# Image sums, spectra's first steps, the image load and the attention's add moved inside layer 0 of a two-layer Fourier and attention kernel

## The chip, the cores and the metric

The kernel runs on one core of one Trainium2 chip. The metric is device microseconds of one execution, given as the median of several runs. The profile is of one further execution.

## The reference

All data is float32; x is (4, 32, 128, 128). Two layers are added to x one after the other. Only the first concerns the change: it treats each of the 4 batch entries as 32 images of 128x128.

```python
x = x + _L0_conv_ref(_gn(x), ...)        # _gn: group norm over groups of 4 channels, whole batch entry
# inside _L0_conv_ref, xa = _gn(x) as 128 images of 128x128:
xn = _inorm(xa, norm1_w, norm1_b)        # _inorm: mean and variance of each image
k = _fno_layer(xn, Kcw, Ksw, Hs, Ws)     # truncated FFT, mode weights, inverse FFT, plus a skip
q = _fno_layer(xn, Qcw, Qsw, Hs, Ws)
v = _fno_layer(xn, Vcw, Vsw, H, W)
p_attn = softmax(q·k / sqrt(Hs*Ws))      # over the 32 images of a batch entry, per head
av = p_attn · v
p = _fno_layer(av, Pcw, Psw, H, W)
a = _inorm(p + xa, attn_w, attn_b)
an = _inorm(a, norm2_w, norm2_b)
m = _fno_layer(an, m0cw, m0sw, H, W, inner_norm=True, act=True)    # gelu
m = _fno_layer(m, m1cw, m1sw, H, W, inner_norm=True, act=False)
out = _inorm(m, mon_w, mon_b) + a
# second layer: t += attention(layer_norm(t)); t += mixture of 8 experts, top 2 (layer_norm(t))
```

## The kernel before

`layer0` runs over the four batch entries b, with the 32 images of one entry in SBUF as `xt`, 128 partitions (rows) by 32 x 128. FFTs are matmuls with cosine and sine tables. Means and variances are not taken from the images where their spectrum or sums give them, so that each normalisation becomes a scale and a bias of some later operation.

The body of iteration b has these stages, in the order of the program:

- **Load** of images b+1 (`load`, L122): four DMAs of 512 KB, two issued by SyncE (SP), two by ScalarE (ACT), at the head of the iteration. The pool `l0_x` has two buffers.
- **Value product** (L756 to L788): five blocks of columns of the modes (`NK` = 13 of 64 each). In a block, four pairs of DMAs on SP fetch `xb` (the spectra, replicated over partitions by a broadcast from DRAM; 8 DMAs of 214.5 KB to a block in all but the last, four buffers); POOL and DVE multiply by the weights `gb` (`u`, L773 and L775), and PE sums into `po`. After each block ACT copies `po` to `rs` (L788). Then `py` and `inverse` bring the result to image space and add it to `q`.
- **Statistics of q** (`stats`, `flat_part`, L831): mean and variance, and `q_r`, the inverse deviation, by `inv_std` (L204): Ln and Exp on ACT (L208, L209) between small DVE operations. `ra` is the scale of q, `r2` that of the second normalisation.
- **spectra(0, q)** (L852): `first_step` (PE `pz`, evacuated to `z1` by `evacuate`, L188 on ACT two times in three and L190 on DVE), then PE `px` (L871), `sqx` on ACT (L873), `part1`, `part2` on DVE (L879, L882), their sum on POOL (L885), a negated copy on ACT (L891).
- **v0's chain** (`weighed`, L894): the squares times a weight (L899), their row sum (L906), two small operations (L909, L915), a matmul `ms` with a matrix of ones; then `r0` by `inv_std`, and the scales `hq`, `hs0`, `hb` of gelu.
- **back(0)** (L290, twice, a half of the images each): PE `y1` (L297), evacuation `v1`, PE `four` (L308), and for each image `gelu`: DVE L941, ACT Gelu L944, DVE `bn_stats` L951. Behind each half, `add_attention` for 16 images: one DVE operation each (L848), `xr = q * ra + xr`, on the image tile of b itself.
- **image_sums(b+1)** (L320): squares of the images on ACT, row sums and square sums on PE (`rows8`, L330, 16 pairs of matmuls), `ev`, 16 small matmuls `s12`, then a chain of small operations over DVE, PE (`mg`, `bg`, `my`) and ACT (`gn_r`, `n1_r`, each an Ln and an Exp): group norm's scale and shift, and the first instance norm's scale `ysc`.
- **spectra(1, gl)** and **spectra_of_images(b+1)** (L418): for groups of 8 images a `first_step`, the correction for the group's mean (`less_mean`, two DVE operations), `px` (L263, L264) with the columns `colg` that hold the group norm's scale, `xx` on DVE, stores to `xd` by SP; at the end `xm` (ACT, L457).
- **v1's chain**, as v0's, to the scales `c2`, `c3` and the bias `cq`.
- **attention_weights(b+1)** (L491): 17 steps of products `pa` (DVE) and `pb` (DVE one time in three, else POOL L524, 12 of 17) and PE `sp`, then `spt`, scores, softmax, and `pr` by way of DRAM, with which the next value product begins.
- **The end of b**: ACT scales gelu's result (L999, Identity with a scale and a bias, 32 images), POOL adds four groups of 8 images to `xr` (L1006), `back(spec, a, last)` adds the rest, SP stores.

For b = 0 the image sums, the spectra and the attention weights run ahead of the loop, beside the preparation of the value weights. In the last iteration there is no next batch; the first part of layer 1 is begun in its place.

PSUM tiles have the tags `a`, `b` and `wide`, of two buffers each: `pz`, `po` and `pxt` are `a`; `px`, `py`, `sk` and `four` are `b`; `y1`, `xw`, `m`, `x0`, all `sums` and `rows8` are `wide`. In SBUF, tag `z` has two buffers, `pr` six.

The order within layer 0 isn't written by hand: a planner places each engine's instructions from the program's order, the dependencies and its own estimates of their durations. Once placed, each engine runs its instructions strictly in that order. Layer 1's attention is in an order written out by hand.

Of the kernel before, what the change touches and what calls it, by code (L numbers as in the profile page):

```python
# [13 lines left out]
P = 128  # L14
# [94 lines left out]
def layer0(  # L109
# [9 lines left out]
    ]  # L119
    const, ps, images, values, modes = (p.__enter__() for p in pools + right)  # L120

    def load(b):  # L122
        xt = images.tile([P, T, C], F32, name=f"x_{b}", tag="x")
        for g in range(0, T, GI):
            eng = nc.sync if g % 16 == 0 else nc.scalar
            eng.dma_start(out=xt[:, g : g + GI], in_=x[b, g : g + GI].rearrange("t w c -> w t c"))
        return xt

    def logarithms():
# [120 lines left out]
            if z.shape[2] > P:  # L250
                evacuate(z[:, k : k + 4, P:], pz[:, :, :64], -1.0)

    def forward(images, c1, c2, take, change):


        n = c1.shape[1]
        z = grp.tile([P, GI, 192], F32, name="z", tag="z")
        first_step(images, z)
        change(z)
        for k in range(0, GI, 4):  # L260
            px = ps.tile([P, 4, n], F32, name="px", tag="b")
# [46 lines left out]
            nc.tensor.matmul(four, inv, v, start=True, stop=True)  # L308
            take([image(a, g, k) for k in range(4)], four)

    def sums(name, matrix, src):

        m = ps.tile(list(src.shape), F32, name=name, tag="wide")
        nc.tensor.matmul(m, matrix, src, start=True, stop=True)
        return m

# [3 lines left out]
    def image_sums(b, xt):  # L320


        rows8 = ps.tile([64, 4, C], F32, name="rows8", tag="wide")
        for g in GROUPS:
            xx2 = grp.tile([P, GI, C], F32, name="xx2", tag="pr", bufs=6)
            nc.scalar.activation(xx2, xt[:, g : g + GI], AF.Square)
            for h in range(2):
                m = g // 4 + h
                for k, src in enumerate((xt[:, 4 * m : 4 * m + 4], xx2[:, 4 * h : 4 * h + 4])):
                    nc.tensor.matmul(  # L330
                        rows8[32 * k : 32 * k + 32],
                        one_of_8[:, 7 - m : 39 - m],
                        src,
                        start=m == 0,
                        stop=m == 7,
                    )
        ev = grp.tile([64, 4, C], F32, name="ev", tag="v", bufs=3)
        nc.scalar.copy(ev, rows8)
        s12 = ps.tile([P, 2, 512], F32, name="s12", tag="wide")[:, :, :T]
        for j in range(4):  # L340
            for k in range(2):
                r = slice(32 * k, 32 * k + 8)
                nc.tensor.matmul(s12[:, k, j::4], ev[r, j], ident[r, r], start=True, stop=True)
        sv = small.tile([P, 2, T], F32, name="sv", tag="pk_sq")
        nc.vector.tensor_copy(sv, s12)

        tot = one("tot", 2)
        nc.vector.tensor_reduce(tot, sv, AX.X, ALU.add)
        mg = sums("mg", group, tot)
        gm = one("gm")  # L350
        nc.vector.tensor_copy(gm, mg[:, 0:1])
        gv = one("gv")
        nc.vector.tensor_mul(gv, gm, gm)
        nc.vector.tensor_tensor(gv, mg[:, 1:2], gv, ALU.subtract)
        gr, _ = inv_std("gn_r", gv, 1)
        gs = one("gs")
        nc.vector.tensor_mul(gs, gm, gr)

        both = small.tile([P, 2, 32], F32, name="both", tag="both")
        nc.vector.tensor_scalar(both[:, 0], of_group, gr, None, ALU.mult)  # L360
        nc.vector.tensor_scalar(both[:, 1], of_group, gs, -1.0, ALU.mult, ALU.mult)
        by_group = small.tile([P, 2, 32], F32, name="by_group", tag="by_group")
        nc.vector.tensor_copy(by_group, sums("bg", ones, both))
        n = 1 + 2 * KY
        colg = small.tile([P, 2, n], F32, name="colg", tag="colg")
        nc.vector.tensor_scalar(colg[:, 0], cols1[:, :n], gr, None, ALU.mult)
        nc.vector.tensor_scalar(colg[:, 1], cols2[:, :n], gr, None, ALU.mult)
        m128 = one("m128")
        nc.vector.tensor_scalar(m128, gm, 128.0, None, ALU.mult)

        gs128 = one("gs128")
        nc.vector.tensor_scalar(gs128, gs, 128.0, None, ALU.mult)
        gg = one("gg")
        nc.vector.tensor_mul(gg, gs, gs128)
        gr2 = one("gr2")
        nc.vector.tensor_mul(gr2, gr, gr)
        grs = one("grs")
        nc.vector.tensor_scalar(grs, gs, gr, -2.0, ALU.mult, ALU.mult)
        y12 = small.tile([P, 2, T], F32, name="y12", tag="pk")
        nc.vector.tensor_scalar(y12[:, 0], sv[:, 0], gr, gs128, ALU.mult, ALU.subtract)  # L380
        nc.vector.tensor_scalar(y12[:, 1], sv[:, 1], gr2, gg, ALU.mult, ALU.add)
        nc.vector.scalar_tensor_tensor(
            y12[:, 1], sv[:, 0], grs, y12[:, 1], ALU.mult, ALU.add
        )
        nc.vector.tensor_scalar(y12, y12, 1.0 / NPIX, None, ALU.mult)
        my = sums("my", ones, y12)
        ym, yv = per_image("ym"), per_image("yv")
        nc.vector.tensor_copy(ym, my[:, 0])
        nc.vector.tensor_mul(yv, ym, ym)
        nc.vector.tensor_tensor(yv, my[:, 1], yv, ALU.subtract)  # L390
        yr, _ = inv_std("n1_r", yv)
        ysc = scalars(ALU.mult, "n1_s", yr, par[:, N1W : N1W + 1])
        return by_group, colg, m128, ysc

    prep_pool = tc.tile_pool(name="l0_prep", bufs=1)
    prep = prep_pool.__enter__()
# [21 lines left out]
    def spectra_of_images(b, xt, normed):  # L418


        _, colg, m128, ysc = normed
        n = 1 + 2 * KY
        xx = modes.tile([P, T, n], F32, name=f"xx_{b}", tag="xx")
        xd = dram.tile([T, 2, KX, KY], F32, name=f"xd_{b}")
        for g in GROUPS:

            def scaled(k, px):
                i = slice(g + k, g + k + 4)
                nc.vector.tensor_tensor(
                    xx[:, i], px, ysc[:, i].unsqueeze(2).to_broadcast([P, 4, n]), ALU.mult  # L430
                )

            def less_mean(z):
                nc.vector.tensor_scalar(z[:, :, 0], z[:, :, 0], m128, None, ALU.subtract)
                nc.vector.tensor_scalar(z[:, :, P], z[:, :, P], m128, None, ALU.add)

            forward([xt[:, g + t] for t in range(GI)], colg[:, 0], colg[:, 1], scaled, less_mean)

            i = slice(g, g + GI)

            for r, y in ((0, 1 + KY), (64, 1)):
                bias = par[r : r + 1, N1B : N1B + 1].to_broadcast([1, GI])
                nc.vector.tensor_copy(xx[r : r + 1, i, y], bias)
            for part in range(2):
                nc.sync.dma_start(
                    out=xd[i, part].rearrange("t x y -> x t y"),
                    in_=xx[64 * part : 64 * part + 64, i, 1 + KY :],
                )
# [238 lines left out]
    for b in range(B):  # L687
        xt = loaded
        by_group, _, _, ysc = normed
        xd = front[2]  # L690
        if b + 1 < B:
            loaded = load(b + 1)

        ph, pr = weights


# [54 lines left out]
        for x0 in range(0, KX, NK):  # L751
# [3 lines left out]
            for i in range(4):  # L755
                xb = late.tile([P, 2, NK * KY], F32, name="xb", tag="xb")[:, :, :m]  # L756
                for r in range(2):
                    nc.sync.dma_start(
                        out=xb[:, r],
                        in_=xd[8 * i : 8 * i + 8, r, x0 : x0 + nk]  # L760
                        .rearrange("s x y -> s (x y)")
                        .unsqueeze(1)
                        .to_broadcast([8, 16, m]),
                    )
# [20 lines left out]
                if i % 2 and at_c < C:  # L785
                    skips(at_c)
                    at_c += 16
            nc.scalar.copy(rs[:, x0 : x0 + nk].rearrange("p x y -> p (x y)"), po)  # L788
        if b + 1 == B:
            for p in reversed(right):  # L790
                p.__exit__(None, None, None)
# [52 lines left out]

        def add_attention(g):

            for t in range(g, g + GI):
                nc.vector.scalar_tensor_tensor(  # L848
                    xr[:, t], q[:, t], ra[:, t : t + 1], xr[:, t], ALU.mult, ALU.add
                )  # L850

        def spectra(layer, src):  # L852

# [78 lines left out]
        nc.vector.tensor_scalar(hb, hb, par[:, S0 : S0 + 1], None, ALU.mult)  # L932
        nc.vector.tensor_mul(dq, dq, hs0)
        nc.vector.tensor_tensor(hb, hb, dq, ALU.add)
        gl = big.tile([P, T, C], F32, name=f"g_{b}", tag="y")
        st = grp.tile([P, T, 6], F32, name="st", tag="st")
        for a in HALVES:
# [13 lines left out]
                    nc.vector.bn_stats(st[:, t], gl[:, t])  # L951

            back(spec, a, gelu)
            for g in (16 * a, 16 * a + GI):
                add_attention(g)

        logarithms()
        if b + 1 < B:
            normed = image_sums(b + 1, loaded)
        else:  # L960
            first((ps, images))

        glm, glv, flat = stats("gl", st)
# [1 line left out]
        dg = per_image("dq")  # L965
        nc.vector.tensor_copy(dg, d1)
        spec, sq = spectra(1, gl)
        if b + 1 < B:
            front = spectra_of_images(b + 1, loaded, normed)
        v1 = weighed("v1", sq, squares, layers[1][2])  # L970
# [675 lines left out]
```

## Time and profile before

| what | us |
| --- | --- |
| median of 3 runs | 3180.41 |
| lowest and highest | 3179.98, 3183.43 |
| profiled execution, its own time | 3191.62 |
| its span in the trace | 3189.9 |
| busy PE / DVE / ACT / POOL | 2928.7 / 2290.9 / 2311.7 / 2102.7 |
| mean granted TensorE clock | 0.953 |

In the profile, L12 is line 12 of the kernel before. "PE" are matmuls, "PEld" the loads of their weights, DVE is VectorE, ACT ScalarE, POOL GpSimd. Tenths of busy time are given for 40 equal slices of the span; "PEclk" is the clock that the throttle granted to TensorE, in tenths of full speed. In brackets behind an instruction stands how long its engine was idle before it, and what released it; "x16" are 16 instructions in a row of one line. The arrow in `out<-in` leads from the operands to the result.

### The profile page before, as it was taken

The page shows a single profiled execution, that of the slowest core. Times are in us where ns is not written, and L with a number is a line of the kernel's source. Part 1 is how long each engine was busy: PE and PEld are TensorE (multiplying, and loading weights), DVE is VectorE, ACT ScalarE, POOL GpSimd, SP SyncE. Part 2 cuts the span into 40 slices and gives each one's busy share as a digit, 9 for nine tenths or more (in the row PEclk, how much of TensorE's full clock was granted, in tenths as well). Part 3 has the DMA queues.
Part 4 walks back from the last instruction along what each step waited for, and adds up shares of the span by engine and source line. Part 5 has one row for each costly group of instructions (what it writes and reads, how often), then busy time and mean ns, then how long its engine had stood idle before and what let it go on. Part 6 is the DMA issues. An engine that isn't in the chain of part 4 may idle for free.

```text
span 3189.9 us, 53099 instructions
## 1 busy us (share of the span) xinstructions
PE 2928.7 (92%) x19634; PEld 1438.2 (45%) x19634; DVE 2290.9 (72%) x5035; ACT 2311.7 (72%) x3138; POOL 2102.7 (66%) x1831
## 2 busy tenths in 40 slices
PE   7888798798888789999999999999999999999997
PEld 5366365345546444444344443444444444444443
DVE  5876666667677566777666868866778777687887
ACT  2344243253343589998999999998999999999992
POOL 1621540460451289878788797889878889888773
PEclk6998998899898799999999999999999999999998
DMA  6301310130140211010111010011010011101000
GB/s 140 111 18 30 95 50 3 49 123 1 30 130 2 57 31 31 8 31 7 31 37 24 14 24 14 8 39 31 23 29 9 14 37 24 37 1 31 14 14 14
DMA packets 152308, 112.77 MB, mean 35 GB/s; under 512 B 36878, under 2 KB 140657, under 8 KB 151441
## 3 DMA queue, kind: packets, MB, share of 16 engines
q1 hardware_dynamic: 136209, 103.61, 12.2%
q10 hardware_dynamic: 15840, 5.77, 0.8%
q8 instruction: 155, 2.54, 0.3%
q14 instruction: 104, 0.85, 0.1%
HBM read 68.37 MB, written 20.00 MB: 28 GB/s over the span
## 4 chain that ended last, share of the span: by engine, by line
PE 61%; POOL 12%; ACT 9%; DVE 9%; issue 7%; DMA 1%; ACTq 0%; POOLq 0%; DVEq 0%; SPq 0%
PE d L1446 19%; PE po L1465 11%; PE px L1352 6%; ACT r L1496 4%; PE po L778 4%; PE n L1446 3%; POOL e L1505 3%; POOL e L1504 3%; PE pz L248 2%; PE four L308 2%; ACT e L1512 2%; PE px L871 1%; PE sk L742 1%; POOL kx L1111 1%; DVE r L1501 1%
## 5 line engine op out<-in xcount | busy, mean ns | idle before, releaser
L1501 DVE TENSOR_TENSOR r<-n,r 128x1024 f32<-128x1024 f32 (+1 forms) x1056 | 961.6, 952 | 479.0 <-PE n L1446 389.4
L1504 POOL TENSOR_TENSOR e<-r 128x512 f32<-128x512 f32 x528 | 673.2, 1275 | 268.1 <-DVE r L1501 267.6
L1496 ACT ACTIVATE r<-d 128x1024 f32<-128x1024 f32 (+1 forms) x1056 | 792.9, 802 | 67.4 <-PE n L1446 56.4
L1508 ACT ACTIVATE r<-r 128x1536 f32<-128x1536 f32 x528 | 783.6, 1484 | 16.8
L1505 POOL TENSOR_TENSOR e<-e,r 128x512 f32<-128x512 f32 x528 | 671.3, 1271 | 41.4
L1446 PE MATMUL d<-qe,ke 32*128 32x512 f32 (+3 forms) x2304 | 605.8, 602 | 39.6 <-ACT r L1496 36.5
L1465 PE MATMUL po<-e,kx 128*128 128x512 f32 (+3 forms) x1152 | 594.5, 605 | 15.6 <-POOL e L1517 15.6
L1446 PE MATMUL n<-qe,ke 32*128 32x512 f32 (+3 forms) x2304 | 606.2, 601 | 0.0
L1446 PE MATMUL n<-qf,kf 32*128 32x512 f32 (+3 forms) x2304 | 552.6, 554 | 0.0
L1446 PE MATMUL d<-qf,kf 32*128 32x512 f32 (+3 forms) x2304 | 550.2, 553 | 0.0
L1356 DVE SCALAR_TENSOR_TENSOR xc<-px,wgt,xc 128x128 f32<-128x128 f32 x1024 | 358.1, 350 | 42.2 <-PE px L1352 9.7
L1512 ACT ACTIVATE e<-e 128x512 f32<-128x512 f32 x528 | 325.8, 617 | 66.2 <-POOL e L1505 65.6
L1465 PEld LDWEIGHTS po<-e,kx 128*128 128x128 f32 x1152 | 175.5, 188 | 392.8 <-issue 306.9
L1446 PEld LDWEIGHTS d<-qe,ke 32*128 32x128 f32 x2304 | 176.5, 183 | 359.3 <-ACT r L1496 339.5
L773 POOL TENSOR_TENSOR u<-xb,gb 128x858 f32<-128x858 f32 (+1 forms) x120 | 233.1, 1968 | 139.5 <-PE po L778 128.0
L1446 PEld LDWEIGHTS d<-qf,kf 32*128 32x128 f32 x2304 | 220.2, 186 | 176.1 <-issue 163.8
L1352 PE MATMUL px<-we,x2t 128*128 128x512 f32 x512 | 264.0, 601 | 6.8 <-DVE xc L1356 6.0
L775 DVE TENSOR_TENSOR u<-xw,gb 128x858 f32<-128x858 f32 (+1 forms) x200 | 206.6, 1082 | 59.2 <-PE po L778 46.6
L885 POOL TENSOR_TENSOR spec<-part,part 128x512 f32<-128x512 f32 x16 | 24.8, 1550 | 333.4 <-ACT z L188 75.2
L1446 PEld LDWEIGHTS n<-qf,kf 32*128 32x128 f32 x2304 | 228.3, 185 | 19.2 <-issue 11.4
L778 PE MATMUL po<-u,pr 128*32 128x429 f32 (+1 forms) x1280 | 191.1, 548 | 26.8 <-DVE u L775 11.7
L524 POOL TENSOR_TENSOR pb<-xm 128x1024 f32<-128x1024 f32 x48 | 90.7, 1913 | 159.1 <-ACT xm L457 152.8
(388 smaller groups left out, 3953.9 us busy)
## 6 DMA issues: line engine op xcount, KB each, us to landing
xb<-xd SPq DMA_DIRECT2D x128, 214.5 KB
xc<-x SPq DMA_DIRECT2D x29, 512.0 KB
x<-x SPq DMA_DIRECT2D x16, 512.0 KB
qf<-qe SPq DMA_DIRECT2D x64, 128.0 KB
out<-xc SPq DMA_DIRECT2D x15, 512.0 KB
xb<-xd SPq DMA_DIRECT2D x32, 198.0 KB
gb<-gd SPq DMA_DIRECT2D x4, 1056.0 KB
x<-in_x SPq DMA_DIRECT2D x8, 512.0 KB
```

Of the source, the lines that this page charges most:

```text
L773: nc.gpsimd.tensor_tensor(u, xb, gk, ALU.mult)
L778: nc.tensor.matmul(po[32 * j : 32 * j + 32], pr[:, i, k], u[:, r], start=i == 0 and k == 0, stop=i == 3 and k == 1,)
L1352: nc.tensor.matmul(px, x2t[:, k * P : (k + 1) * P], we[:, e0 : e0 + 4], start=True, stop=True)
L1356: nc.vector.scalar_tensor_tensor(xc[:, k], px[:, e], wgt[:, k, e0 + e : e0 + e + 1], xc[:, k], ALU.mult, ALU.add)
L1446: nc.tensor.matmul(o, k, q, start=turn == 0 or g > 0, stop=turn == 1 or g > 0)
L1465: nc.tensor.matmul(sums[c, h][:, q0 : q0 + c1 - c0], kx[:, jb], e[:, c0:c1], start=jb == 0, stop=is_last and q0 > 2 * P, skip_group_check= ...
L1496: nc.scalar.activation(r[:, g], d, AF.Ln, scale=1.0 / DSCALE)
L1501: nc.vector.tensor_tensor(r[:, g], part, r[:, g], ALU.mult)
L1504: nc.gpsimd.tensor_tensor(e, r[:, 1], r[:, 2], ALU.add)
L1505: nc.gpsimd.tensor_tensor(e, e, r[:, 0], ALU.add)
L1508: nc.scalar.activation(r, r, AF.Exp, scale=-1.0)
L1512: nc.scalar.activation(e, e, AF.Exp)
```

## The change

- `image_sums(b+1)` is called before gelu's stage, behind v0's chain in the program. Its PSUM tiles take the tags `a` and `b` instead of `wide`, and `s12` becomes two tiles, copied by two operations.
- The four DMAs that load images b+1 are issued in the second of the value product's five blocks, all on SP, with an ordering dependency behind the last broadcast of that block.
- In `spectra_of_images` the first step of a group of 8 images is put ahead of the `px` of the group before it. The correction for the mean is one DVE operation for a group instead of two.
- `add_attention` becomes, for 8 images, eight scaled copies on ACT and one addition on POOL. Its calls stand behind `spectra(1, gl)`, where the program had them behind each half of gelu's stage.

```diff
-    def load(b):
+    def load(b, behind=None):
...
-            eng = nc.sync if g % 16 == 0 else nc.scalar
-            eng.dma_start(out=xt[:, g : g + GI], in_=x[b, g : g + GI].rearrange("t w c -> w t c"))
+            eng = nc.sync if behind is not None or g % 16 == 0 else nc.scalar
+            d = eng.dma_start(
+                out=xt[:, g : g + GI], in_=x[b, g : g + GI].rearrange("t w c -> w t c")
+            )
+            if behind is not None:
+                tc.add_manual_dep(
+                    d.ins,
+                    behind.ins.name,
...
-    def forward(images, c1, c2, take, change):
+    def forward(z, c1, c2, take):
...
-        z = grp.tile([P, GI, 192], F32, name="z", tag="z")
-        first_step(images, z)
-        change(z)
...
-    def sums(name, matrix, src):
+    def sums(name, matrix, src, tag="wide"):
...
-        rows8 = ps.tile([64, 4, C], F32, name="rows8", tag="wide")
+        rows8 = ps.tile([64, 4, C], F32, name="rows8", tag="a")
...
-        s12 = ps.tile([P, 2, 512], F32, name="s12", tag="wide")[:, :, :T]
+        s12 = [ps.tile([P, T], F32, name=f"s{t}", tag=t) for t in "ab"]
...
-        nc.vector.tensor_copy(sv, s12)
+        for k in range(2):
+            nc.vector.tensor_copy(sv[:, k], s12[k])
...
-        mg = sums("mg", group, tot)
+        mg = sums("mg", group, tot, "a")
...
-        m128 = one("m128")
-        nc.vector.tensor_scalar(m128, gm, 128.0, None, ALU.mult)
+        shift = one("shift", 2)
+        for k in range(2):
+            nc.vector.tensor_scalar(shift[:, k : k + 1], gm, 256.0 * k - 128.0, None, ALU.mult)
...
         xd = dram.tile([T, 2, KX, KY], F32, name=f"xd_{b}")
-        for g in GROUPS:
+        steps = []
+        for g in (*GROUPS, None):
+            if g is not None:
+                z = grp.tile([P, GI, 192], F32, name="z", tag="z")
+                first_step([xt[:, g + t] for t in range(GI)], z)
+                nc.vector.tensor_tensor(
+                    z[:, :, ::P], z[:, :, ::P], shift.unsqueeze(1).to_broadcast([P, GI, 2]), ALU.add
+                )
+                steps.append((g, z))
+                if g == 0:
+                    continue
+            g, z = steps.pop(0)
...
-            def less_mean(z):
-                nc.vector.tensor_scalar(z[:, :, 0], z[:, :, 0], m128, None, ALU.subtract)
-                nc.vector.tensor_scalar(z[:, :, P], z[:, :, P], m128, None, ALU.add)
-
-            forward([xt[:, g + t] for t in range(GI)], colg[:, 0], colg[:, 1], scaled, less_mean)
+            forward(z, colg[:, 0], colg[:, 1], scaled)
...
         xd = front[2]
-        if b + 1 < B:
-            loaded = load(b + 1)
...
-                    nc.sync.dma_start(
+                    broadcast = nc.sync.dma_start(
                         out=xb[:, r],
...
             nc.scalar.copy(rs[:, x0 : x0 + nk].rearrange("p x y -> p (x y)"), po)
+            if x0 == NK and b + 1 < B:
+                loaded = load(b + 1, broadcast)
...
         def add_attention(g):
-            for t in range(g, g + GI):
-                nc.vector.scalar_tensor_tensor(
-                    xr[:, t], q[:, t], ra[:, t : t + 1], xr[:, t], ALU.mult, ALU.add
-                )
+            part = grp.tile([P, GI, C], F32, name="scaled_q", tag="pr", bufs=6)
+            for t in range(GI):
+                nc.scalar.activation(
+                    part[:, t], q[:, g + t], AF.Identity, scale=ra[:, g + t : g + t + 1]
+                )
+            nc.gpsimd.tensor_tensor(xr[:, g : g + GI], xr[:, g : g + GI], part, ALU.add)
...
         nc.vector.tensor_tensor(hb, hb, dq, ALU.add)
+        if b + 1 < B:
+            normed = image_sums(b + 1, loaded)
...
             back(spec, a, gelu)
-            for g in (16 * a, 16 * a + GI):
-                add_attention(g)
 
         logarithms()
-        if b + 1 < B:
-            normed = image_sums(b + 1, loaded)
-        else:
+        if b + 1 == B:
             first((ps, images))
...
         spec, sq = spectra(1, gl)
+        for g in GROUPS:
+            add_attention(g)
```

More of the change, by code (lines that the diff above doesn't have):

```diff
@@ L120, in layer0 @@
     const, ps, images, values, modes = (p.__enter__() for p in pools + right)
-    def load(b):
+    def load(b, behind=None):
         xt = images.tile([P, T, C], F32, name=f"x_{b}", tag="x")
         for g in range(0, T, GI):
-            eng = nc.sync if g % 16 == 0 else nc.scalar
-            eng.dma_start(out=xt[:, g : g + GI], in_=x[b, g : g + GI].rearrange("t w c -> w t c"))
+            eng = nc.sync if behind is not None or g % 16 == 0 else nc.scalar
[6 more added lines that the diff above has]
+                    behind.ins.name,
+                    mybir.DependencyInfo(mybir.DependencyClass.NoSync, mybir.DependencyReason.DATA),
+                    reason="order",
+                )
         return xt
@@ L309, in back @@
             take([image(a, g, k) for k in range(4)], four)
-    def sums(name, matrix, src):
-        m = ps.tile(list(src.shape), F32, name=name, tag="wide")
+    def sums(name, matrix, src, tag="wide"):
+        m = ps.tile(list(src.shape), F32, name=name, tag=tag)
         nc.tensor.matmul(m, matrix, src, start=True, stop=True)
@@ L342, in image_sums @@
                 r = slice(32 * k, 32 * k + 8)
-                nc.tensor.matmul(s12[:, k, j::4], ev[r, j], ident[r, r], start=True, stop=True)
+                nc.tensor.matmul(s12[k][:, j::4], ev[r, j], ident[r, r], start=True, stop=True)
         sv = small.tile([P, 2, T], F32, name="sv", tag="pk_sq")
-        nc.vector.tensor_copy(sv, s12)
+        for k in range(2):
+            nc.vector.tensor_copy(sv[:, k], s12[k])
         tot = one("tot", 2)
         nc.vector.tensor_reduce(tot, sv, AX.X, ALU.add)
-        mg = sums("mg", group, tot)
+        mg = sums("mg", group, tot, "a")
         gm = one("gm")
@@ L362, in image_sums @@
         by_group = small.tile([P, 2, 32], F32, name="by_group", tag="by_group")
-        nc.vector.tensor_copy(by_group, sums("bg", ones, both))
+        nc.vector.tensor_copy(by_group, sums("bg", ones, both, "a"))
         n = 1 + 2 * KY
@@ L385, in image_sums @@
         nc.vector.tensor_scalar(y12, y12, 1.0 / NPIX, None, ALU.mult)
-        my = sums("my", ones, y12)
+        my = sums("my", ones, y12, "a")
         ym, yv = per_image("ym"), per_image("yv")
@@ L392, in image_sums @@
         ysc = scalars(ALU.mult, "n1_s", yr, par[:, N1W : N1W + 1])
-        return by_group, colg, m128, ysc
+        return by_group, colg, shift, ysc
     prep_pool = tc.tile_pool(name="l0_prep", bufs=1)
@@ L418, in spectra_of_images @@
     def spectra_of_images(b, xt, normed):
-        _, colg, m128, ysc = normed
+        _, colg, shift, ysc = normed
         n = 1 + 2 * KY
```

## The prediction

> **What bounds the kernel now.** I read the page's busy tenths first, to see where TensorE is short of work and at which clock.
>
> ```profile
> PE   7888798798888789999999999999999999999997
> ...
> PEclk6998998899898799999999999999999999999998
> ```
>
> A slice is 79.75 us. Layer 0 is the first 14 slices (to 1106 us), where PE stands at 7 to 9 and the clock dips; layer 1 behind it is PE at 9 throughout, and the diff doesn't touch it. So all gain or loss lies in layer 0, between the end of one batch's value product and the start of the next, four times (q_r's Ln at 211.9, 470.4, 738.6, 1001.0 us). Next the windows of image batch 1 (columns: window, length, busy PE, PEld, DVE, ACT, POOL with counts, clock, DMA):
>
> ```profile
> 467.00:487.00 20.00, 13.49 (x152) 10.20 (x152) 17.11 (x60) 5.29 (x14) 3.44 (x2) 0.92 0.01 1
> 487.00:495.00 8.00, 6.18 (x70) 4.60 (x70) 6.58 (x33) 2.46 (x5) 0.00 (x0) 0.71 0.01 2
> 495.00:522.00 27.00, 27.00 (x111) 13.78 (x112) 16.27 (x64) 16.86 (x38) 0.00 (x0) 0.64 0.00 1
> 522.00:541.00 19.00, 18.31 (x169) 12.05 (x165) 9.79 (x51) 5.56 (x13) 1.27 (x1) 1.00 0.01 1
> 541.00:573.00 32.00, 28.61 (x226) 26.82 (x227) 19.33 (x64) 6.71 (x18) 1.27 (x1) 0.89 0.22 50
> 573.00:610.00 37.00, 27.79 (x174) 7.36 (x174) 28.43 (x34) 15.41 (x37) 33.30 (x17) 0.77 0.07 21
> ```
>
> In the first, PE waits and DVE is full; in the third PE is full at clock 0.64; the last is POOL's. The chain of waits for 467 to 573 says which piece ends each (start, length, what):
>
> ```profile
> 482.38 1.13 DVE sqx L899
> 483.51 1.27 DVE x L848
> 484.77 1.13 DVE v_r L906
> 486.75 0.65 PE ms L314 x2
> 488.68 0.78 DVE x L848 x3
> ...
> 519.10 5.27 PE rows L330 x22
> ```
>
> The attention's adds (L848) stand inside v0's chain, and the next batch's row sums (L330) inside gelu's stretch. The timelines of PE, POOL and ACT price the wait, the lock and what follows:
>
> ```profile
> 486.75 0.63 PE L314 MATMUL ms<-v_s,ones 128*128 128x32 f32 x2 [6.33 <-DVE v_s L915]
> 482.46 2.17 POOL L885 TENSOR_TENSOR spec<-part,part 128x512 f32<-128x512 f32 x1 [6.09 <-DVE part L882]
> 488.72 0.23 ACT L208 ACTIVATE r<-r_ve 128x32 f32<-128x32 f32 x1 [3.64 <-DVE r_ve L207]
> 492.99 1.08 ACT L188 ACTIVATE v<-y 128x512 f32<-128x512 f32 x2 [3.78 <-DVE v L190]
> 524.46 0.58 ACT L338 COPY ev<-rows 64x512 f32<-64x512 f32 x1 [1.66 <-PE rows L330]
> 537.81 0.22 ACT L208 ACTIVATE n_r<-n_r_ve 128x32 f32<-128x32 f32 x1
> ```
>
> **What the Trainium skill says.** "SBUF — State Buffer", "SBUF: two separate sides": a GpSimd operation and a VectorE operation with two SBUF inputs exclude each other. The trace agrees: L885 took 2.17 us where it met L899, 1.27 otherwise. "TensorE: Matmul & The Clock Gate", "Part 1: The HAM clock gate": the clock halves after an idle window and returns after about 3.4 us of sustained work. It agrees at 484 to 514; it doesn't at 32 to 66, where PE was busy with px and stayed at 0.5. "DMA: Bandwidth & Descriptors", "Issuing engines are not separate DMA queues": transfers of SP and ACT share the 16 engines. It agrees: batch 2's image load, half on each, delayed the xb behind it to 384.4 us.
>
> **The change, part by part.** The instruction order of the changed program shows where things stand. Batches 0, 1, 2 have all parts.
>
> *A, q_r to the first gelu* (25.7, 25.0, 26.0 us now). Removed: the 32 L848, 0.26 us apart on DVE; some 5 fall inside v0's links, about 1.4 us. Added on ACT: 32 copies. L999 with two pointers took 12.04/31 = 0.39 us each; by "ScalarE: Activation LUTs", "What ACT_TABLE_LOAD costs", a pointer less saves 0.09, so 0.30 to 0.39, 9.6 to 12.4 us; I take 12.4. ACT is busy 5.3 of 20 there, so 17.7 of 20: it fits, but sqx waits up to four copies (1.6 us), and r0's Ln stands behind all. Added on POOL: four adds, as L1006 2.36 us each, 9.4 us beside its 3.4; each can hold L899 or L909 up to 2.4 us. I take ms 2 us late, range 0 to 5. Then the image-sum chain: in the new ACT order ev, gn_r's and n1_r's Ln and Exp stand ahead of v1's first evacuation (L188) and the table load, and on DVE the chain's small operations ahead of its own share. ev to n1_r took 13.35 us above, of which about 4.3 were waits for foreign work on PE and DVE, so 9.1 alone. r0's Ln to evacuation took 4.3; now 9.1 + 0.5. So +5 more: **+7 a batch**, 4 to 10.
>
> *B, gelu's stretch* (19.2, 26.1, 19.0). The rows8 passes leave; 13 of 16 pairs now come ahead of ms, in the 6.3 us where PE waited (16 x 0.43 = 6.9). B1 lost most by half clock. −1, −6, −1, together **−8**, range −13 to −4.
>
> *C, last gelu to xm* (49.9, 51.4, 52.4). Gone: rows8's tail (1.3 to 3 us), ev and the sums' waits between spectra(1)'s passes: in batch 3, where nothing is interleaved, spectra(1) ends 17.8 us after gelu, against about 20. The images' transform then runs one group ahead, so px doesn't wait for its group's evacuation: 28.6 of 32 us were busy at clock 0.89, leaving 4 to 7. The mean's correction becomes one DVE operation in place of two, ahead of need. 2 + 4 + 5 = **−11 a batch**, range −13 to −8.
>
> *D, xm to spt to po* (36.8 + 27 to 30). POOL's ten pb products precede L1006, so they aren't held 2 x 2.36 us; but the last two stand behind the first L1006, which needs cq, whose chain on DVE moved behind xx. **+0.5 a batch**, range −3 to +2.5.
>
> *E, the load.* Four DMAs move, all on SP, behind the 16 broadcasts of the second K block; ACT's queue loses two. Batch 2's load cost the first xb 9.8 us in the chain at 375.9, part of it covered: that block ended 13.6 us after the start against 14.35 a block later. The load's 2.1 MB moves to the third block's broadcasts, prefetched further. −1.5 in batches 1 and 2; +1.5 in batch 0, where x_1 was loaded at the start. **−1.5**, range −6 to +6. The image sums have it from a block or more before they start.
>
> *F, batch 3*: no sums, only the swap of adds: A's part without the chain, **+2**, range −3 to +4.
>
> *G, the start.* The sums take PSUM's "a" and "b", so 64 passes that ran in the chain's waits (16 to 31 us) follow `my` (35.2): 64 x 0.116 = 7.4 us at full clock. px at half clock (32 to 66) would gain as much if these warm it; 16 passes of 8 images' px take 3.5 us against 6.8. Also x_1's half load leaves ACT's queue. **−2**, range −8 to +9.
>
> Sum: 21 − 8 − 33 + 1.5 − 1.5 + 2 − 2 = −20 us. The profiled execution had a span of 3189.9 and 3191.62 in all, so 3171.6 by its own clock; it lies 11.2 above the median of 3180.41, so **3160** there. The ends of A to G taken as independent: 9, 4.5, 7.5, 8, 6, 3.5, 8.5 in squares, about 18 us either way.
>
> **Rivals.**
> *R1, slower: the copies on ACT become the bound of part A.* If none of the 12.4 us hides (the copies run while sqx, spec and z1's evacuations are wanted), A is 12.4 + 6 = 18.4 a batch. The other parts give −41, so the sign turns at 13.7, and 0.2% slower from 15.8. At 18.4: +14, 3195. For it: ACT executes in order and r0's Ln stands last. Against it: ACT was idle 14.7 of the 20 us.
> *R2, no difference: part C isn't realised.* If PE, no longer held by the chain, waits for z's evacuation instead (L188 already ended 14.1 us of waits in 467 to 573), C is −4, and the sum +1: 3181. D at its upper end does half of this. Against it: DVE and ACT were 19 and 7 busy of 32.
> *R3, more:* the start warms and A is at its low end: −35, 3145.
> That the change doesn't do what it says is nearly excluded by the order; only the place of rows8's last three pairs is against the words.
>
> **The numbers.** Likeliest case 0.55, R3 0.12, R2 0.17, R1 0.16. About 0.2% (6.4 us) is what a measurement of this kernel can tell from no change. The likeliest and R3 are faster, with a quarter of R2: 0.71. R2's middle is same: 0.10. R1 and the rest slower: 0.19. The range 3138 to 3190 leaves out the lower half of R3 and the upper half of R1.
>
> **What would show it.** After: ms's idle below 6.3 us, with rows8 ahead of it; gelu's first activation 32 us after q_r's Ln (25 now); gelu's stretch near 19 in batch 1; last gelu to xm near 40; POOL's pb without a gap; the second K block's broadcasts without a 9.8 us piece. Wrong if the scaled copies end the wait of r0's Ln by several us (R1), if gelu to xm stays at 47 or more (R2), or if layer 1's part, 2084 us from 1106 to the end, changes by over 5.

## The result, and the profile after

The changed kernel is slower: a median of 3225.45 us (3219.59 to 3227.78, 4 runs) against 3181.92 us (4 runs) for the kernel before, a ratio of 1.0133 with a 95% interval of 1.0116 to 1.0151. The profiled execution of after took 3227.78 us, its span is 3226.1; the two spans differ by 36.2 us, somewhat less than the medians, since the profiled execution of before lay 11 us above its own median. Layer 1 took 2088.8 us from its table load at 1137.3 to the end, 2088.9 before (from 1101.0). So all of it is in layer 0.

The starts and ends of the stages, read from the timelines of both (the tiles named in the left column), give one table. The stages are those of the prediction; each cell is us before → after.

| stage | batch 0 | batch 1 | batch 2 | batch 3 |
| --- | --- | --- | --- | --- |
| start to first po | 113.8 → 109.0 | | | |
| po to its last `rs` (value product) | 67.8 → 72.1 | 68.8 → 71.7 | 68.9 → 71.9 | 68.7 → 67.6 |
| A: q_r's Ln to first gelu | 25.7 → 37.3 | 24.9 → 35.4 | 26.0 → 39.1 | 24.6 → 25.2 |
| B: first to last gelu | 19.2 → 20.1 | 26.1 → 22.3 | 19.0 → 17.5 | 20.8 → 21.9 |
| C: last gelu to xm | 49.9 → 31.4 | 51.4 → 34.1 | 52.4 → 40.5 | |
| D: xm to spt (attention's products) | 36.8 → 47.5 | 36.8 → 47.7 | 36.8 → 47.6 | |
| spt to next po | 28.0 → 31.7 | 29.3 → 32.5 | 25.9 → 35.5 | |

From the last `rs` to q_r's Ln it is 30 to 34 us, the same in both kernels. C gave 47.7 us over three batches. A took 35.2, D 32.4, the stage behind D 16.5, the value product 10.2; the start gave 4.8 back, B 4.4.

The busy tenths of after, in 40 slices of 80.65 us, show little of this, because the longer stages aren't idle ones:

```profile
PE   7788898788789789999998999999999999999997
...
PEclk8898898898889699999999999999999999999998
```

The windows of the stages of batch 1 show it (columns as before: window, length, busy PE, PEld, DVE, ACT, POOL, clock, DMA). The first line is the kernel before, in the stage behind D, which the prediction did not show; the others are the kernel after, two of stage A, then B, C, D and the stage behind it:

```profile
610.00:639.00 29.00, 19.34 (x152) 8.78 (x150) 18.10 (x47) 5.69 (x11) 2.59 (x2) 0.92 0.27 69
```
```profile
478.00:498.00 20.00, 18.75 (x180) 12.82 (x180) 13.47 (x40) 12.13 (x38) 8.20 (x4) 1.00 0.00 1
498.00:517.00 19.00, 13.45 (x96) 8.72 (x96) 13.13 (x55) 6.73 (x20) 4.67 (x2) 0.63 0.00 1
517.00:539.00 22.00, 20.93 (x122) 14.12 (x120) 16.26 (x64) 16.15 (x39) 0.00 (x0) 0.78 0.00 1
539.00:573.00 34.00, 32.14 (x322) 29.33 (x322) 19.88 (x55) 9.25 (x19) 2.53 (x2) 1.00 0.17 39
573.00:621.00 48.00, 29.74 (x174) 6.53 (x176) 39.97 (x55) 11.28 (x28) 27.36 (x14) 0.87 0.08 22
621.00:653.00 32.00, 24.95 (x154) 11.79 (x152) 17.89 (x45) 10.66 (x24) 8.69 (x5) 0.71 0.24 60
```

C is now PE's at full clock: 32.1 of 34 us busy. In D it is no longer POOL that is full, but DVE: 40.0 of 48 us, and it was 28.4 of 37. The last two rows are the loss that the prediction did not have.

**Stage D.** Who waits for whom in 573 to 621 (columns: waiting engine, tile and line, what it waited for, us in total, times, longest):

```profile
PEld sp L543 <- DVE pa L537: 21.3, 13, 3.6
ACT g L1015 <- DVE cq L1008: 18.2, 1, 18.2
POOL pb L539 <- PE sp L543: 15.0, 4, 6.5
```

PE's `sp` waits for DVE's products, and POOL, which was the bound, waits 15 us for PE. DVE's timeline says why it is late (start, length, engine, line, operation, tile):

```profile
576.06 1.23 DVE L219 TENSOR_TENSOR r_t<-r 128x32 f32<-128x32 f32 x1 [1.78 <-ACT r L218]
577.32 1.83 DVE L220 TENSOR_TENSOR r_t<-r_t,r_ve 128x32 f32<-128x32 f32 x1
...
585.60 2.01 DVE L995 TENSOR_SCALAR vc<-gl_var,par 128x32 f32<-128x32 f32 x1
587.53 1.21 DVE L537 TENSOR_TENSOR pa<-xp,xm 128x1024 f32<-128x1024 f32 x1
588.66 0.83 DVE L996 TENSOR_TENSOR v<-v,vc 128x32 f32<-128x32 f32 x1
...
599.89 1.93 DVE L208 TENSOR_SCALAR c<-rm,par 128x32 f32<-128x32 f32 x1
```

These are v1's chain, r1, rm, c2, c3 and cq, threaded between the products. While POOL runs a pb of 1.9 us, an operation of 0.18 us waits for its end. Ten of them took 0.75 to 2.01 us, 11.8 us in sum where some 2 would do. In the kernel before, the same operations ran ahead of the products and met no pb; these are two of them (L211 and L199 there, L220 and L208 here):

```profile
560.58 0.19 DVE L211 TENSOR_TENSOR r_t<-r_t,r_ve 128x32 f32<-128x32 f32 x1
572.58 0.23 DVE L199 TENSOR_SCALAR c<-rm,par 128x32 f32<-128x32 f32 x1
```

That is 9.8 us on DVE, against 10.9 by which D grew. But it is not the whole cause: the first L1022 (L1006 before) waits for cq, and the last two pb stand behind it on POOL until 618.8, 3.7 us after DVE's last product has ended (0.1 before). Every experiment that shortens D takes away both, so that their shares are read from this trace and not tested apart.

The chain is there because of the order on PE, seen in these lines of DVE and PE, and, last, one of PE in the kernel before:

```profile
556.61 0.24 DVE L931 SCALAR_TENSOR_TENSOR v_s<-flat,column,v_s 128x32 f32<-128x32 f32 x1
```
```profile
572.14 0.36 PE L320 MATMUL ms<-v_s,ones 128*128 128x32 f32 x2
```
```profile
558.82 0.31 PE L314 MATMUL ms<-v_s,ones 128*128 128x32 f32 x2
```

v_s was ready at 556.9, but the planner had placed v1's `ms` behind all the image transform's `px`, so it ran 15 us later. Before, `ms` ran among those `px`, 4 us after v_s.

**Stage A**, its two new delays, from the timelines of DVE, POOL and PE; first the same two operations of DVE in the kernel before:

```profile
487.79 0.18 DVE L924 TENSOR_TENSOR v<-v,r 128x32 f32<-128x32 f32 x1
488.15 0.18 DVE L925 TENSOR_TENSOR v<-v,r 128x32 f32<-128x32 f32 x1
```
```profile
498.26 2.15 DVE L940 TENSOR_TENSOR v<-v,r 128x32 f32<-128x32 f32 x1
500.44 2.28 DVE L941 TENSOR_TENSOR v<-v,r 128x32 f32<-128x32 f32 x1
```
```profile
498.00 4.67 POOL L866 TENSOR_TENSOR x<-x,scaled_q 128x1024 f32<-128x1024 f32 x2 [1.11 <-ACT scaled_q L863]
```
```profile
509.62 0.66 PE L320 MATMUL bg<-both,ones 128*128 128x64 f32 x2 [1.06 <-DVE both L368]
510.21 1.23 PE L303 MATMUL y<-cst,spec 32*128 32x128 f32 x14
511.81 0.66 PE L320 MATMUL my<-y,ones 128*128 128x64 f32 x2 [0.37 <-DVE y L393]
512.40 1.23 PE L303 MATMUL y<-cst,spec 32*128 32x128 f32 x12
```

Each of v0's two multiplications behind `ms` waits out one of POOL's two last additions: 4.4 us in place of 0.4. And the passes of gelu's own `y1` stand in PE's queue between the image sums' matmuls; the last twelve stand behind `my`, near the end of that chain.

### The profile page after: what moved, and what is told of

Its sections match the earlier page's. It is cut to its first block, busy times and chain, and to the rows that moved or that the text cites. A ratio compares the mean times of both kernels' runs of the same rounds, so it can differ in the third digit from the quotient of the medians.

```text
span 3226.1 us, 53098 instructions
## 1 busy us (share of the span) xinstructions
PE 2938.0 (91%) x19634; PEld 1426.6 (44%) x19634; DVE 2304.2 (71%) x4899; ACT 2348.3 (73%) x3266; POOL 2140.0 (66%) x1847
## 4 chain that ended last, share of the span: by engine, by line
PE 50%; POOL 10%; ACT 9%; DVE 7%; issue 6%; DMA 0%; POOLq 0%; DVEq 0%; SPq 0%; ACTq 0%
PE d L1462 18%; PE po L1481 10%; PE px L1368 6%; ACT r L1512 5%; PE n L1462 3%; POOL e L1521 3%; POOL e L1520 3%; PE po L790 2%; ACT e L1528 2%; DVE r L1517 1%; POOL kx L1127 1%; POOL x L1127 1%; DVE xc L1372 1%; PE four L314 1%; PE pz L257 1%
## 5 line engine op out<-in xcount | busy, mean ns | idle before, releaser
L1372 DVE SCALAR_TENSOR_TENSOR xc<-px,wgt,xc 128x128 f32<-128x128 f32 x1024 | 358.3, 350 | 42.2 <-PE px L1368 9.7
L790 PE MATMUL po<-u,pr 128*32 128x429 f32 (+1 forms) x1280 | 198.6, 554 | 32.3 <-DVE u L787 14.4
```

Source lines behind the costliest of these rows:

```text
L790: nc.tensor.matmul(po[32 * j : 32 * j + 32], pr[:, i, k], u[:, r], start=i == 0 and k == 0, stop=i == 3 and k == 1,)
L1372: nc.vector.scalar_tensor_tensor(xc[:, k], px[:, e], wgt[:, k, e0 + e : e0 + e + 1], xc[:, k], ALU.mult, ALU.add)
```

## The experiments

All ratios are to the kernel before on the same chip. The stages named A to D are those of the table.

**v1's chain ahead of the image transform** (on the kernel after):

```diff
-            front = spectra_of_images(b + 1, loaded, normed)
         v1 = weighed("v1", sq, squares, layers[1][2])
...
         nc.vector.tensor_tensor(cq, cq, dg, ALU.add)
+        if b + 1 < B:
+            front = spectra_of_images(b + 1, loaded, normed)
```

> The kernel after, with the twenty-odd operations from v1's chain to cq written ahead of spectra_of_images in the program, so that the planner places them before the image transform. Theory 1 (the chain of r1, rm and cq, placed behind the transform and threaded between the attention's products, costs the time): xm to spt falls from 47.6 us to 36 to 39 in each of three batches, spt to the next value product from 32 to about 28, in all 35 to 50 us off, 3175 to 3190. Theory 2 (the attention stage is long because POOL and ACT carry the new add and a later load): xm to spt stays above 45 and the time within 8 us of 3225.

Measured: 3198.5 us, 1.0057 (1.0040 to 1.0073). D is 34.4, 38.4 and 37.0 us, the stage behind it 28.1, 29.2 and 34.6. Theory 1's mechanism holds for D; its sum was too high by 8 us and more. C became 5.3, 6.2 and 0.9 us longer: the chain's `ms` now stand among the transform's passes. And the stage behind D of batch 2 kept its 34.6 us, at a clock of 0.65, though D was short.

**First steps not ahead** (on the kernel after; the correction remains one operation):

```diff
-        for g in (*GROUPS, None):
...
-            g, z = steps.pop(0)
+        for g in GROUPS:
+            z = grp.tile([P, GI, 192], F32, name="z", tag="z")
+            first_step([xt[:, g + t] for t in range(GI)], z)
```

> The kernel after, with the first step of a group of images again directly before its own px (the one-operation correction stays). Theory 1: cq is ready before the attention's products again, so xm to spt returns to about 37 us (-11 a batch) and spt to the value product to 28 (-5), while gelu to xm loses the part of its gain that was due to the order, 3 to 7 us a batch: 3190 to 3205. Theory 2: xm to spt stays above 45 us, gelu to xm grows, 3235 to 3245.

Measured: 3202.2 us, 1.0064 (1.0049 to 1.0079). D 38.2, 36.0, 36.7; behind it 28.0, 29.4, 27.5; C 37.2, 40.4, 44.0. As theory 1 had it: the order of the first steps is what displaced v1's chain. Without that order D and the stage behind it are 47 us shorter in sum, and C 16 longer.

**The image load at its old place** (on the kernel after):

```diff
+        if b + 1 < B:
+            loaded = load(b + 1)
...
-            if x0 == NK and b + 1 < B:
-                loaded = load(b + 1, broadcast)
```

> The kernel after, with the image load at the head of the iteration, on both queues, as before. Theory 3 (in the third block the load delays broadcasts that are needed at once): the value product returns from 72 to 69 us in batches 1 and 2 and from 72 to 65 to 68 in batch 0: 6 to 10 us off, 3215 to 3219. Rival (the load costs the same wherever it lies, and the product is long for another reason, such as POOL's late start): the product stays at 71 to 72 us, within 3 us of 3225.

Measured: 3226.07 us, 1.0138 (1.0121 to 1.0154). The product returned to 67.5, 69.1 and 70.1 us, as expected. The time did not: the first value product began at 113.4 again in place of 109.0, and C of batch 2 took 43.2. The move of the load costs about 9 us in the products and gives 4.4 at the start; what is left of it doesn't show in the time.

**The attention's add on DVE again, in its old place** (on the kernel after):

```diff
             back(spec, a, gelu)
+            for g in (16 * a, 16 * a + GI):
+                add_attention(g)      # L848 of the kernel before
...
-        for g in GROUPS:
-            add_attention(g)
```

> The kernel after, with the attention's add on DVE again, behind each half of gelu's stage. Theory 4 (half of the 10 to 13 us by which gelu starts later comes from ACT's copies and POOL's adds, half from the image sums' chain): q_r's Ln to gelu falls from 37.4, 35.5, 39.2 to about 31 us, 15 to 20 us off, 3205 to 3210. Rival (it is the image sums' chain alone): the stage stays within 2 us of now, and DVE's 32 operations return in v0's chain, within 5 us of 3225.

Measured: 3196.97 us, 1.0055 (1.0038 to 1.0071). A fell to 31.7, 30.2 and 32.6 us, 5.2 to 6.5 less, and from `ms` to r0's Ln it took 2.2 us in place of 5.4. Theory 4 holds for the stage: half of the delay was ACT's and POOL's new work. The median fell by 28 us, the profiled execution by 22. A gives 17 of these; C of batch 2 was 10 us shorter (30.5 for 40.5, at a clock of 1.00 for 0.92) and B in sum 5 longer, which the edit does not explain by itself.

**First steps ahead alone** (on the kernel before: `spectra_of_images`, `forward` and `shift` as in the change):

```diff
+        steps = []
+        for g in (*GROUPS, None):
...
+            g, z = steps.pop(0)
```

> The kernel before with only the new order of spectra's first steps and the one-operation correction. Theory 1 (this part alone makes the planner put v1's ms behind the image transform): xm to spt 46 to 48 us in place of 36.8, spt to the value product +3 to +6, gelu to xm 4 to 8 us less than its 50 to 52: 3195 to 3215, slower. Rival (the late chain needs the other parts as well, such as the early sums): xm to spt stays at 37 and the kernel is 10 to 20 us faster than before.

Measured: 3201.27 us, 1.0067 (1.0040 to 1.0093). D 46.9, 46.3, 46.8, C 43.4, 46.0, 45.4. This one part makes the loss in D, without the others. The profiled execution is the fastest of the four, 3190.55 us, and in it C and B give back what D loses; the median is 18 us above before. Behind D only 0.6 to 1.3 us were added, not 3 to 6: the larger growth there in the kernel after goes with TensorE's clock (below).

**Image sums early alone** (on the kernel before: the call ahead of gelu's stage, PSUM tags a and b):

```diff
+        if b + 1 < B:
+            normed = image_sums(b + 1, loaded)
         gl = big.tile([P, T, C], F32, name=f"g_{b}", tag="y")
```

> The kernel before with only image_sums ahead of gelu's stage, in PSUM tags a and b. Theory 4 (the sums' chain delays gelu by about 6 us a batch, and saves rows8 in gelu's stretch and 10 us behind it): q_r to gelu 31 to 33 us, gelu to xm 37 to 41, xm to spt unchanged at 37; 3165 to 3180. Rival (the chain costs as much as it saves): within 6 us of before.

Measured: 3170.89 us, 0.9967 (0.9957 to 0.9977). A 31.8, 30.1, 32.1; C 40.4, 42.0, 34.6; D 36.8, 36.0, 37.0. The time is as expected, and so are the stages but for C of batches 1 and 2 and A of batch 1, which lie 1 to 2 us outside: this part of the change is a gain, of 12 us.

**Attention's add on ACT and POOL alone** (on the kernel before; `add_attention` and its calls as in the change):

```diff
+            nc.gpsimd.tensor_tensor(xr[:, g : g + GI], xr[:, g : g + GI], part, ALU.add)
```

> The kernel before with only the attention's add on ACT and POOL, behind spectra(1) in the program. Theory 7 (POOL's additions hold v0's small operations on DVE, ACT's copies stand before r0's Ln): ms to r0's Ln grows from 2.0 to about 5.4 us and q_r's Ln to gelu from 25.5 to about 28 to 31; the rest unchanged: 8 to 16 us slower. Rival (the copies and additions hide beside v0's chain, and DVE is relieved of 32 operations): 0 to 5 us faster.

Measured: 3196.72 us, 1.0057 (1.0037 to 1.0078). A 28.7, 27.8, 30.7, 3 to 5 us longer, but not all where they were expected: `ms` to r0's Ln took 1.6, 3.3 and 3.3, and `ms` itself came up to 3 us later. In the profile this is 11 us; the medians differ by 18.

**Both faults out: v1's chain first, the add on DVE** (on the kernel after, the first and fourth edit above together):

> The kernel after with both faults taken out: v1's chain ahead of the image transform in the program, and the attention's add on DVE behind each half of gelu's stage. If the two effects add, 27 and 28 us off 3225: 3168 to 3176, faster than before; gelu 30 to 33 us after q_r, xm to spt 35 to 39. If they share a cause, 3190 to 3198.

Measured: 3175.14 us, 0.9981 (0.9967 to 0.9995). The two effects add, and the change is then a gain, though a small one. A is still 31.7, 30.2 and 32.1 us.

**As that, with powers on POOL for the sums' two inverse deviations**:

```diff
-        gr, _ = inv_std("gn_r", gv, 1)
+        gr, _ = (pow_std if b else inv_std)("gn_r", gv, 1)
...
-        yr, _ = inv_std("n1_r", yv)
+        yr, _ = (pow_std if b else inv_std)("n1_r", yv)
# pow_std: ve = var + 1e-5 on DVE, then nc.gpsimd.tensor_tensor(r, ve, nhalf.to_broadcast([P, n]), ALU.pow)
```

> As v1_dve, with the two inverse deviations of the image sums of batches 1 to 3 by one power operation on POOL each, in place of Ln, Exp and four DVE operations. Theory 5 (what remains of gelu's delay is ACT's order: gn_r's and n1_r's Ln and Exp ahead of v1's evacuations and the table load): r0's Ln to gelu falls from 12 to 7 to 8 us, 12 to 15 us off v1_dve. Rival (DVE's share of the chain, not ACT's order, holds the evacuations): within 4 us of v1_dve.

Measured: 3186.0 us, 1.0009 (0.9998 to 1.0019): worse. r0's Ln to gelu grew to 15.4, 15.7 and 15.3 us. The timelines of POOL, PE and ACT of this kernel, in batch 0:

```profile
231.94 0.58 POOL L333 TENSOR_TENSOR gn_r<-gn_r_ve,nhalf 128x1 f32<-128x1 f32 x1 [7.89 <-DVE gn_r_ve L332]
237.13 5.43 POOL L333 TENSOR_TENSOR n_r<-n_r_ve,nhalf 128x32 f32<-128x32 f32 x1 [4.61 <-DVE n_r_ve L332]
```
```profile
235.49 0.66 PE L320 MATMUL my<-y,ones 128*128 128x64 f32 x2 [0.51 <-DVE y L403]
236.08 0.81 PE L303 MATMUL y<-cst,spec 32*128 32x128 f32 x8
```
```profile
236.92 1.08 ACT L197 ACTIVATE v<-y 128x512 f32<-128x512 f32 x2 [8.06 <-PE y L303]
```

Theory 5 falls. With the chain's Ln and Exp off ACT, the evacuation of v1 still waited 8 us, and for PE: `y1`'s last eight passes stand behind `my`. And a power of 32 columns on POOL took 5.43 us, for which DVE then waited with the evacuations behind it.

**v1's chain behind the attention's products** (on the kernel after):

```diff
+        if b + 1 < B:
+            weights = attention_weights(b + 1, front)
         v1 = weighed("v1", sq, squares, layers[1][2])
```

> The kernel after, with v1's chain to cq written behind attention_weights, so that all 22 of DVE's products precede it and all of POOL's 12 pb precede the additions. Theory 6 (the attention stage is long because the chain's small operations, threaded between the products, are held by POOL's pb: in the kernel after ten of them took 0.75 to 2.0 us in place of 0.2, about 10 us in sum): xm to spt falls from 47.6 to 30 to 34 us, spt to the value product grows by 3 to 8, since ACT's 32 copies and POOL's four additions now fall there: 15 to 35 us off 3225. Rival (a late cq costs its lateness wherever it stands): the two stages together stay at 79 to 83 us and the time within 8 us of 3225.

Measured: 3188.73 us, 1.0032 (1.0016 to 1.0049), 37 us below after, by the medians of different chips. D is 30.4, 29.8 and 30.4 us; the stage behind it 36.5, 38.2 and 37.3, 1.8 to 5.7 longer. In the timelines of POOL and DVE the products now follow one another, and the chain behind them is fast:

```profile
570.54 7.53 POOL L539 TENSOR_TENSOR pb<-xm 128x1024 f32<-128x1024 f32 x4 [1.92 <-PE sp L543]
```
```profile
593.80 0.19 DVE L220 TENSOR_TENSOR r_t<-r_t,r_ve 128x32 f32<-128x32 f32 x1
600.84 0.18 DVE L221 TENSOR_SCALAR rm_t<-rm_t 128x32 f32<-128x32 f32 x1
```

So a late cq alone does not make D long: here it is later still. It was the threading of the chain, and of the addition that waits for it, between DVE's and POOL's products. D is even shorter than in the kernel before (36.8), since POOL's four additions left it too.

**The image sums in three parts** (on the kernel with the sums early alone): row sums and `ev` before gelu's stage, the chain behind its first half, n1_r behind its second.

```diff
-            normed = image_sums(b + 1, loaded)
+            ev = image_rows(b + 1, loaded)          # up to ev
...
+            if a == 0 and b + 1 < B:
+                part = image_chain(b + 1, ev)       # s12 to yv; gn_r by pow_std
...
+        if b + 1 < B:
+            normed = image_scale(part)              # n1_r, ysc
```

> b_sums with the image sums in three parts: row sums and ev ahead of gelu's stage as there, the chain from s12 on behind gelu's first half (gn_r by one power operation on POOL, one column, so that no table is loaded between), n1_r behind gelu's second half. Theory 8 (gelu's delay of 6 us in b_sums comes from the chain's matmuls ahead of y1's last passes in PE's queue): q_r's Ln to gelu returns to 25 to 27 us, gelu's stretch 20 to 24, last gelu to xm 36 to 42: 10 to 20 us below b_sums, 3150 to 3162. Rival (the chain costs as much wherever it stands): gelu's stretch or the stage behind it grows by 5 us, within 5 us of b_sums.

Measured: 3156.0 us, 0.9929 (0.9914 to 0.9944): the fastest version, 22.6 us below before. A is back at 24.3, 25.9 and 23.4 us, since the `y1` of the first half runs in one piece; in this kernel's timeline of PE:

```profile
482.91 2.07 PE L297 MATMUL y<-cst,spec 32*128 32x128 f32 x64
```

B took 28.7, 23.9 and 20.3, C 36.5, 42.2 and 44.7. Theory 8 holds for A. The rival was right in part: against the kernel with the sums early alone B grew by 6 and 5 us in batches 0 and 1, and C by 10 in batch 2, so that of the 20 us that A gave 15 were spent again in B and C. Each against before on its own chip, the split gained 22.6 us and the early sums 12.0.

**The same on v1's chain first, the add on DVE, the load at the head** (the kernel with both faults out):

> As b_split, on the kernel v1_dve with the image load at the head of the iteration: it has the early first steps of spectra, the one-operation correction, and v1's chain ahead of the transform. If the early first steps are worth something once v1's chain isn't late, 2 to 8 us below b_split; if the planner's order gives it back, within 3 us of it.

Measured: 3164.08 us, 0.9954 (0.9939 to 0.9970), not below the version before it but 8 us above. Neither expectation came true. D 35.6, 38.1, 37.4 and C 36.1, 47.4, 39.6 show no gain from the early first steps.

## Why the prediction was wrong

It forecast 3160 us, between 3138 and 3190; it was 3225. The terms of its sum, against the same stages:

| part | forecast | measured |
| --- | --- | --- |
| A, three batches | +21 | +35.2 |
| B | −8 | −4.4 |
| C | −33 | −47.7 |
| D with the stage behind it | +1.5 | +48.9 |
| E, the load (value products of 0 to 2) | −1.5 | +10.2 |
| F, batch 3 | +2 | −1.0 |
| G, the start | −2 | −4.8 |

**The step that failed is D.** It named the fact, "cq, whose chain on DVE moved behind xx", and priced only the two pb behind the first L1006, at 0.5 us a batch. It did not count the threaded operations themselves, though it had the price in hand: the exclusive lock of the Trainium skill's "SBUF — State Buffer", section "SBUF: two separate sides", and L885 at 2.17 us. That lock was applied in A, to L899 and L909, and not here, where twenty-five small operations are threaded beside twelve pb of 1.9 us; in batch 1 ten of them were held, for 9.8 us. And the two pb that it did price ended 3.7 us behind DVE's last product. The kernel with only the early first steps shows the loss alone (46 to 47 us), and the one with the chain behind the products shows it gone (30). By the experiments the attention's add weighs as much in the time: 27 us come back with v1's chain first, 28 with the add on DVE, 50 with both. D is the term that the prediction put at nearly nothing; the add it priced too low, in A.

About a third of the 48.9, the 16.5 us behind D, is of another kind. Two lines of the chain that ended last in 621 to 654 of the kernel after, and the same passes before:

```profile
622.24 1.84 PE sc L562 x2
624.08 1.84 PE sc L555 x2
```
```profile
610.37 1.05 PE sc L547 x2
611.41 0.97 PE sc L540 x2
```

TensorE's clock was 0.72, 0.71 and 0.64 for this stage, against 1.00, 0.92 and 1.00 before. Two windows of the kernel after show where it fell (columns as above):

```profile
584.90:618.80 33.90, 20.93 (x124) 3.06 (x116) 30.11 (x35) 7.88 (x21) 21.39 (x12) 1.00 0.00 1
618.90:636.00 17.10, 17.10 (x81) 7.96 (x82) 3.98 (x6) 7.30 (x17) 6.47 (x3) 0.50 0.09 9
```

It was full for 34 us of D, in which PE often waited, fell some 2 us before D ended, and stayed at half for 17.1 us in which PE was busy throughout. The Trainium skill's "TensorE: Matmul & The Clock Gate", "Part 1: The HAM clock gate", has full speed return after about 3.4 us of sustained work; this does not fit that. Nor did it in the stretch for which the prediction said that it fits, 484 to 514 of the kernel before: the clock fell there in an idle stretch, as the page says, but from 494 to 511 PE was busy throughout at a clock of 0.51. And the loss isn't tied to D's length: with the first steps ahead alone D was as long and the clock behind it 0.92, 0.83 and 1.00, and with v1's chain first D of batch 2 was short and the clock 0.65. So the cause of these 16.5 us stays open; it is not shown that the threading in D brought them about.

**A's size was wrong by two terms.** The path from `ms` to r0's Ln grew by 3.4 us in each batch, 10.2 in all, because two of v0's multiplications met POOL's additions; the prediction had the lock at L899 and L909, both ahead of `ms`, and not behind it. And r0's Ln to gelu grew by 6.9 to 7.6, not 5, because the chain holds PE's `y1` passes as well, where the prediction saw ACT's and DVE's order alone. ACT's copies took 0.39 us each and L999, with a pointer more, 0.48: the 0.09 us that the prediction gave to a pointer are there, and ten in a row took 3.0 us, so that 32 take 9.6, the low end of the prediction's range and not the 12.4 that it took. R1, the rival on the slower side, made ACT's copies the bound of A, up to 18.4 us; A grew by 12, and before r0's Ln ACT waited 2.7 us for DVE, not for its copies.

**E failed in its sign.** The broadcasts of the third block are needed at once: from 392 to 428 us of after, ACT waited for them (columns: what it waited for, us in total, times, longest).

```profile
ACT xw L779 <- DMA xb<-xd: 4.7, 3, 3.3
```

The 9.8 us of before, at the head of the product, had mostly been covered, as its short first block said. Together with G the move cost little, and with the load back at its old place the time was the same.

**Right** were the signs and places of A, B and C. C's 12 to 18.5 us a batch look better than forecast (11), but that is the other side of D's loss: with v1's chain back in its place C gave 13.2, 11.1 and 11.0 us, almost exactly the forecast. R2, that C isn't realised, was wrong. G's sign was luck in part: with the load back and the sums still early the first product began at 113.4 us (113.8 before), so the gain at the start came from the load, which the prediction named last, and not from the earlier sums. Of the marks set down beforehand, "POOL's pb without a gap" failed most plainly: gaps of 2.4 to 6.5 us.

## What to carry to other kernels

When a change moves a chain of small operations, find what now stands beside it on the two engines that exclude each other (here VectorE and GpSimd), and price those that can meet it at up to the length of the other engine's operation, not at their own. An order that fills one engine's gaps can push a short but early matmul (here `ms`) behind a long block; in a kernel that a planner orders, read where each chain's first step lands, not only the steps that were moved. And a chain that is put into another's wait must not share an in-order queue with what ends that wait: splitting it, so that only its bulk fills the wait, gave 22.6 us where the whole gave 12.0.

## What the runs showed of the hardware

A VectorE operation of 0.18 us took up to 2.28 us beside GpSimd additions of 2.36 us, and 2.01 us beside products of 1.9 us even where it had only one tensor operand besides its per-row scalars (L995, L208). A GpSimd power took 0.58 us for 128x1 and 5.43 us for 128x32. A VectorE product of 1.21 us, one of whose two tensor operands lies in PSUM (`xp` of `pa`), ran beside the same GpSimd products without growing. TensorE's granted clock stayed at 0.50 for 17.1 us in which it was busy throughout, where passes took 1.84 us in place of 1.05, and had been at 1.00 for 34 us in which it waited for two fifths of the time.
